# Rounding the feed-forward weights in two instructions a block, through 32-bit integers, with six of the second matrix's eight sums on ScalarE

## The chip, the core and the metric

The kernel runs on one core of one Trainium2 chip. A core has five engines that run side by side, each with its own queue of instructions: TensorE (PE in the profile; its weight loads are listed apart as PEld), VectorE (DVE), ScalarE (ACT), GpSimd (POOL) and SyncE (SP), which here only starts transfers. An engine takes its queue in order and waits on semaphores for what others produce. The metric is the device time of one execution in microseconds (us); lower is better.

## The reference

Sixteen sequences of 224 tokens with 512 features go through one gated block: cross-attention to a context of 750 rows per sequence, and then a feed-forward layer whose two weight matrices are rounded to -1, 0 and 1. What matters for this change is the rounding of the weights and where they are used:

```python
def weight_quant(w):
    scale = 1.0 / jnp.clip(jnp.mean(jnp.abs(w)), 1e-05)
    q = jnp.clip(jnp.round(w * scale), -1.0, 1.0) / scale
    return w + jax.lax.stop_gradient(q - w)

def bitlinear(x, w, b):
    xq = act_quant(rmsnorm(x))
    wq = weight_quant(w)
    return jnp.einsum('bsd,fd->bsf', xq, wq) + b
h = bitlinear(x, w1, b1)
h = jax.nn.gelu(h, approximate=False)
return bitlinear(h, w2, b2)

x = x + jnp.tanh(g_xattn[0]) * _L0_xattn_ref(_layernorm(x, axis=-1), ctx_768, mask_BxS2_bk0, ...)
x = x + jnp.tanh(g_ffn[0]) * _L0_ffn_ref(_layernorm(x, axis=-1), ...)
```

`w1` is 2048 x 512 and `w2` is 512 x 2048, both float32. A matrix can be scaled only when the mean of all its absolute values is known.

## The kernel before, in words

With these inputs the kernel takes `compact_path`. Every sequence attends to few context rows; the sequences are sorted by the number of rows that the mask keeps, and only the kept rows are fetched: at most 192 for the first eight sequences and 128 for the other eight (`CAPS`). The main loop at the end of the function runs over the sixteen sequences s. In step s it does the attention of s (`scores`, `turn_probs`, `weighted`), prepares queries, keys and values of s + 1, normalises the tokens of later sequences, and, from s = 2 on, carries pairs of 128-token tiles through the output projection and the feed-forward layer (`residual`, `project`, `normalise`, `up`, `gelu`, `down`). Steps s = 0 and s = 1 have no feed-forward work yet; in its place they prepare the weights, `w1` in step 0 and `w2` in step 1 (`weight_pieces`).

Each matrix is cut into eight blocks of 128 partitions x 1024 values. A block goes through these steps:

- `load_weights`: a transfer of 512 KB on SP's queue into a tile `raw`. There are eight such tiles, so block c of `w2` can be loaded only when block c of `w1` has been rounded out of its tile.
- `sum_weights`: the sum of absolute values of each partition, for even blocks on VectorE (L1363) and for odd ones on ScalarE (L1367). The sums of `w1` are taken ahead of the loop, those of `w2` in step 0, between the roundings of `w1`.
- `scale_weights`, once a matrix: a small matmul with ones adds over the partitions (L1375), and VectorE turns the mean into the scale (L1377 to L1386).
- `round_weights`: VectorE multiplies by the scale and cuts at 1 (L1396), cuts at -1 and writes 16-bit integers, which rounds (L1397), and turns the integers into bfloat16 (L1398). The result `w16` lies in one of three tiles with the tag `xq`.
- `turn_weights`: eight TensorE transposes (L1409 for `w1`, L1413 for `w2`) into PSUM, and an eviction to float8 into `w1T` or `w2T`.

Which engine evicts a PSUM tile is decided while the kernel is built: `evict` (L757 to L766) keeps a running sum of estimated load, `load["v"]` for VectorE and `load["s"]` for ScalarE, and gives the tile to the engine that would end lower. `round_weights` adds 1700 to `load["v"]` for each block; `sum_weights` adds nothing.

`merge` interleaves the three streams of a step (attention, preparation, weights) by their rough costs. From that the framework lays down one fixed queue per engine; neighbours can change places in it, so that in the kernel before the first instruction of block c + 1 stands ahead of the last one of block c. GpSimd's queue holds the normalisation of the tokens (L956 to L961), the fetches of tokens and context rows (L793, L856), two scalings of bias rows (L1519, L1520) and the division of the attention weights by their sum (L1081), which `turn_probs` needs before TensorE can transpose them (L1101).

Of the kernel before, what the change touches and what calls it, by code (L numbers as in the profile page):

```python
# [11 lines left out]
ALU = mybir.AluOpType  # L12
# [713 lines left out]
def compact_path(ctx, tc, sh, x, context, out, late_loads):  # L726

    nc = tc.nc
# [15 lines left out]
    I32 = mybir.dt.int32  # L744
    I16 = mybir.dt.int16
# [7 lines left out]
    load = {"v": 0.0, "s": 0.0}  # L753
# [602 lines left out]
    def sum_weights(wi, c):  # L1356
        if c == 0:
            weight_sums.append(pa.tile([P, NPC], F32, name=f"wsums_{wi}"))
        if c == 1:
            late["junk"] = pa.tile([P, FF], F32, tag="h", name=f"junk_{wi}", bufs=2)  # L1360
        raw = raws[wi, c]
        if c % 2 == 0:
            nc.vector.tensor_reduce(  # L1363
                weight_sums[wi][:, c : c + 1], raw, AX.X, ALU.add, apply_absolute_value=True
            )
        else:
            nc.scalar.activation(late["junk"][:, :W], raw, AF.Abs, accum_out=weight_sums[wi][:, c : c + 1])  # L1367

    weight_scale = [None, None]
# [22 lines left out]
    def round_weights(wi, c):  # L1392

        raw = raws.pop((wi, c))
        quantised[wi, c] = w16 = pa.tile([P, W], BF16, tag="xq", name=f"w16_{wi}_{c}", bufs=3)
        nc.vector.tensor_scalar(raw, raw, weight_scale[wi], 1.0, ALU.mult, ALU.min)  # L1396
        nc.vector.tensor_scalar(w16.bitcast(I16), raw, -1.0, None, ALU.max)  # L1397
        nc.vector.tensor_copy(w16, w16.bitcast(I16))  # L1398
        load["v"] += 1700

    def turn_weights(wi, c):
        w16 = quantised.pop((wi, c))
# [14 lines left out]
    def weight_pieces(wi):  # L1417

        p = []
        if wi == 1:  # L1420
            p += [(0.0, lambda: scale_weights(1))]
        for c in range(NPC + 2):
            if c < NPC:
                p += [(0.2, lambda c=c: round_weights(wi, c))]
                if wi == 0:
                    p += [(0.0, lambda c=c: load_weights(1, c))]
            if c > 1:
                p += [(0.6, lambda c=c: turn_weights(wi, c - 2))]
                if wi == 0:
                    p += [(0.0, lambda c=c: sum_weights(1, c - 2))]  # L1430
        return p
# [51 lines left out]
    with ExitStack() as behind:  # L1483
        for instruction in latest.values():
            behind.enter_context(tc.issue_after(instruction))
        scores(0, 0)
        scores(0, 1)
        for _, piece in queries[3:] + keys_values[3:]:
            piece()
        for c in range(NPC):  # L1490
            sum_weights(0, c)
        scale_weights(0)
        for _, piece in norm_pieces(1):
            piece()
        select(2)

        held = [sh.wo[0:1, 0, 0:1], sh.wo[0:1, 2, 0:1], sh.wo[P // 2 : P // 2 + 1, 2, 0:1]]
        for dst in held + [sh.bo[0:1, 0:1], sh.b1[0:1, 0:1], sh.b2[0:1, 0:1]]:
            nc.scalar.copy(dst, weight_sums[0][0:1, NPC - 1 : NPC])
# [85 lines left out]
```

## Time and profile before

| | |
|---|---|
| three runs | 754.46, 756.20, 758.74 us (median 756.2) |
| the profiled execution | 755.32 us, its span 753.5 us |
| TensorE | 680.1 us busy, 90% of the span |
| VectorE | 505.9 us, 67% |
| ScalarE | 407.6 us, 54% |
| GpSimd | 397.0 us, 53% |
| 43 to 160 us (weights, steps 0 to 2) | TensorE busy 105.3 of 117.0 us |
| 160 to 206 us | TensorE busy 46.0 of 46.0 us |
| 206 us to the end | TensorE busy 497.4 of 547.5 us |

The span runs from the first to the last instruction of the profile; 1.8 us of the execution's time lie around it. All other times here come from that one execution. In a list of instructions a row gives start and duration in us, engine, line, operation, what is written and read with its shape, the count, and in brackets the idle time ahead of it with what ended it. PEclk is the share of its full clock that TensorE was granted. Busy time of TensorE is modelled, so small gaps in it can be missing.

### The profile page before, as it was taken

How to read it: one execution, taken by the hardware profiler on the slowest of the kernel's cores; microseconds unless marked ns; L12 is line 12 of the kernel's file. 1: busy time of each engine (PE TensorE's matmuls, PEld its weight loads, DVE VectorE, ACT ScalarE, POOL GpSimd, SP SyncE). 2: the span in 40 equal slices, each digit the busy share in tenths (PEclk: the TensorE clock that was granted, in tenths of full speed). 3: DMA queues.
4: the chain of work that ended last, by engine and by line, in shares of the span. 5: the costliest groups of instructions: out<-in, count | busy, mean ns of one | idle time of the engine just before them, and what ended most of it. 6: DMA issues, size and time to landing. Idle time of an engine off the chain costs nothing.

```text
span 753.5 us, 11378 instructions
## 1 busy us (share of the span) xinstructions
PE 680.1 (90%) x3902; PEld 432.9 (57%) x3902; DVE 505.9 (67%) x1300; ACT 407.6 (54%) x960; POOL 397.0 (53%) x543
## 2 busy tenths in 40 slices
PE   4997799999999999997999999999999999988652
PEld 3875587666566566555655575666666666443221
DVE  5598765877484784665768676588594939586860
ACT  1556564384663855736657369266565656460530
POOL 6583567464564644647266564565654453536141
PEclk9998999999999999999999999999999999999887
DMA  6874031132223322222142323123122222213150
GB/s 193 314 267 156 11 90 45 15 73 56 69 47 70 82 56 57 67 57 81 28 99 67 71 67 68 32 77 80 58 57 70 56 70 57 71 28 77 35 113 31
DMA packets 87218, 58.77 MB, mean 78 GB/s; under 512 B 75488, under 2 KB 75632, under 8 KB 87024
## 3 DMA queue, kind: packets, MB, share of 16 engines
q1 hardware_dynamic: 79024, 32.00, 18.8%
q0 software_dynamic: 8128, 25.96, 11.1%
q8 instruction: 33, 0.54, 0.3%
q14 instruction: 33, 0.27, 0.1%
HBM read 32.26 MB, written 7.34 MB: 53 GB/s over the span
## 4 chain that ended last, share of the span: by engine, by line
PE 57%; DVE 12%; issue 10%; POOL 9%; DMA 5%; ACT 2%; POOLq 0%; ACTq 0%; DVEq 0%; SPq 0%
PE qp L1008 9%; PE op L1189 9%; PE fp L1304 8%; PE hp L1259 6%; PE kp L892 5%; PE sim L1047 4%; PE vp L907 4%; PE ptp L1101 3%; PE av L1126 3%; DVE a L1282 2%; POOL p L1081 2%; DVE h L1267 2%; DMA raw<-in_L_ffn_w_dram 2%; DMA hqT<-hq 2%; DVE hq L1285 1%
## 5 line engine op out<-in xcount | busy, mean ns | idle before, releaser
L1081 POOL TENSOR_TENSOR p<-p,rec 112x768 f32<-112x768 f32 (+1 forms) x64 | 84.2, 1318 | 74.8 <-DVE rec L1080 29.6
L1304 PE MATMUL fp<-w2T,hqT 128*128 128x512 fp8e4 x448 | 104.2, 387 | 13.8 <-DMA hqT<-hq 13.7
L1259 PE MATMUL hp<-w1T,xqT 128*128 128x512 fp8e4 x448 | 107.0, 383 | 8.8 <-DVE h L1267 6.2
L1071 ACT ACTIVATE p<-p,nm 112x192 f32<-112x192 f32 (+1 forms) x256 | 106.4, 419 | 11.5 <-DVE nm L1061 11.3
L1008 PE MATMUL qp<-xnT,wq_sb 128*128 128x224 f32 x512 | 104.9, 358 | 0.6 <-ACT xnT L766 0.6
L1189 PE MATMUL op<-wo_sb,xoT 128*128 128x512 f32 x224 | 103.7, 599 | 0.0
L1008 PEld LDWEIGHTS qp<-xnT,wq_sb 128*128 128x128 f32 x512 | 96.8, 193 | 6.4 <-issue 3.3
L1267 DVE SCALAR_TENSOR_TENSOR h<-hp,c,b_bc 128x1024 f32<-128x1024 f32 x56 | 71.6, 1280 | 39.9 <-PE hp L1259 37.4
L1061 DVE CUSTOM_DVE_ANT_0 p<-sim,mask 112x192 f32<-112x192 f32 (+1 forms) x256 | 67.7, 319 | 33.9 <-PE sim L1047 33.4
L1304 PEld LDWEIGHTS <-hqT 128*128 128x128 bf16 x448 | 43.3, 99 | 71.0 <-DMA hqT<-hq 16.9
L1282 DVE TENSOR_REDUCE a<-h 128x1 f32<-128x2048 f32 x28 | 63.9, 2282 | 22.4 <-ACT h L1279 22.3
L1259 PEld LDWEIGHTS <-xqT 128*128 128x128 bf16 x448 | 43.2, 98 | 57.7 <-issue 15.4
L1308 DVE SCALAR_TENSOR_TENSOR y<-fp,c,y 128x512 f32<-128x512 f32 x28 | 20.9, 746 | 76.3 <-PE fp L1304 73.0
L1310 POOL DMA_INDIRECT out_dram<-y,token x28 | 30.9, 1104 | 75.6 <-DVE y L1308 70.6
L1290 ACT ACTIVATE h<-h 128x2048 f32<-128x2048 f32 x28 | 53.4, 1907 | 22.1 <-DVE hq L1285 14.7
L1279 ACT ACTIVATE h<-h 128x2048 f32<-128x2048 f32 x28 | 53.5, 1909 | 19.6 <-DVE k L1200 10.6
L1189 PEld LDWEIGHTS op<-wo_sb,xoT 128*128 128x128 f32 x224 | 40.6, 190 | 38.9 <-issue 36.4
L892 PE MATMUL kp<-ctxT,wk_sb 128*128 128x192 f32 (+1 forms) x384 | 60.9, 306 | 0.0
L892 PEld LDWEIGHTS kp<-ctxT,wk_sb 128*128 128x128 f32 x384 | 55.2, 192 | 6.2 <-issue 4.3
L1247 POOL TENSOR_TENSOR y<-y,b_bc 128x512 f32<-128x512 f32 x28 | 36.6, 1311 | 37.9 <-DVE fx L1228 37.6
L766 ACT COPY pT<-ptp 128x448 f32<-128x448 f32 x63 | 32.7, 536 | 42.6 <-PE ptp L1101 41.3
L1101 PE MATMUL ptp<-ident,p 112*128 112x112 f32 x256 | 36.1, 268 | 17.6 <-POOL p L1081 17.5
(165 smaller groups left out, 1191.4 us busy)
## 6 DMA issues: line engine op xcount, KB each, us to landing
raw<-in_L_ffn_w_dram SPq DMA_DIRECT2D x16, 512.0 KB, 5.6
wq_sb<-in_L_xattn_W_q_dram SPq DMA_DIRECT2D x1, 1024.0 KB, 5.8
b_bc<-in_L_ffn_b_dram SPq DMA_DIRECT2D x1, 1024.0 KB, 7.8
wk_sb<-in_L_xattn_W_k_dram SPq DMA_DIRECT2D x1, 768.0 KB, 7.4
wv_sb<-in_L_xattn_W_v_dram SPq DMA_DIRECT2D x1, 768.0 KB, 8.8
wo_sb<-in_L_xattn_W_o_dram SPq DMA_DIRECT2D x1, 512.0 KB, 3.8
wo_sb<-in_L_xattn_W_o_dram SPq DMA_DIRECT2D x2, 256.0 KB, 5.6
x<-in_x_dram,token POOLq DMA_INDIRECT x28, 3.6
```

Source lines behind the costliest of these rows:

```text
L892: nc.tensor.matmul(pk[:, p - p0, :], lhsT=sh.wk[:, c, p * P : (p + 1) * P], rhs=st["ctxT"][:, c, :cap], start=(c == 0), stop=(c == NC - 1),)
L1008: nc.tensor.matmul(pq[:, i, :], lhsT=sh.wq[:, d, (p + i) * P : (p + i + 1) * P], rhs=st["xnT"][:, d, :], start=(d == 0), stop=(d == ND - 1),)
L1061: nc.vector.tensor_tensor_reduce(out=probs[:, h, :cap], in0=sim[:, j, i, :cap], in1=st["mask"][:, j * begin : j * begin + cap], scale=-(DH ...
L1071: nc.scalar.activation(probs[:, h, :cap], probs[:, h, :cap], AF.Exp, bias=nmax, scale=-1.0, accum_out=total[:TQ, h : h + 1],)
L1081: nc.gpsimd.tensor_tensor(probs[:, :, :cap], probs[:, :, :cap], rec[:TQ].unsqueeze(2).to_broadcast([TQ, 4, cap]), ALU.mult,)
L1101: nc.tensor.transpose(pt[:, h, :], probs[:, h, c : c + P], ident[:TQ, :TQ])
L1189: nc.tensor.matmul(po, lhsT=xoT[:, d, at : at + P], rhs=sh.wo[:, d, :], start=(d == 0), stop=(d == ND - 1))
L1259: nc.tensor.matmul(ph[:, n, :], lhsT=f["xqT"][:, k * ND + d, :], rhs=w1T[:, d, at : at + NB], start=(d == 0), stop=(d == ND - 1),)
L1267: nc.vector.scalar_tensor_tensor(h[:, cols], ph.rearrange("t i n -> t (i n)"), f["c1", k], sh.b1[:, cols], ALU.mult, ALU.add)
L1279: nc.scalar.activation(f["h", k], f["h", k], AF.Gelu)
L1282: nc.vector.tensor_reduce(amax[:, k : k + 1], h, AX.X, ALU.max, apply_absolute_value=True)
L1304: nc.tensor.matmul(po, lhsT=f["hqT", k][:, n, :], rhs=w2T[:, n, :], start=(n == 0), stop=(n == NF - 1))
```

## The change

Rounding takes two instructions a block. The first multiplies by the scale and writes the product as 32-bit integers over the block itself, which rounds it; the second reads the integers, cuts them at 1 and at -1 and writes bfloat16. The estimate that `evict` is given falls from 1700 to 1400 a block. For `w2` (`wi == 1`) only blocks 0 and 4 are summed on VectorE; blocks 1, 2, 3, 5, 6 and 7 are summed on ScalarE. For `w1` the division stays as it was, four and four.

```diff
@@ sum_weights
-        if c % 2 == 0:
+        if c % (2 + 2 * wi) == 0:
             nc.vector.tensor_reduce(
                 weight_sums[wi][:, c : c + 1], raw, AX.X, ALU.add, apply_absolute_value=True
             )
@@ round_weights
         raw = raws.pop((wi, c))
         quantised[wi, c] = w16 = pa.tile([P, W], BF16, tag="xq", name=f"w16_{wi}_{c}", bufs=3)
-        nc.vector.tensor_scalar(raw, raw, weight_scale[wi], 1.0, ALU.mult, ALU.min)
-        nc.vector.tensor_scalar(w16.bitcast(I16), raw, -1.0, None, ALU.max)
-        nc.vector.tensor_copy(w16, w16.bitcast(I16))
-        load["v"] += 1700
+        nc.vector.tensor_scalar(raw.bitcast(I32), raw, weight_scale[wi], None, ALU.mult)
+        nc.vector.tensor_scalar(w16, raw.bitcast(I32), 1.0, -1.0, ALU.min, ALU.max)
+        load["v"] += 1400
```

## The prediction

> **What bounds the kernel now.** I read the page first: TensorE is busy 90% of the span, VectorE 67%. So time taken off VectorE counts only where TensorE waits for it. The waits of TensorE from 40 to 206 us are short, and all but the last lie in the weight steps:
>
> ```profile
> PE ptp L1101 <- POOL p L1081: 5.1, 1, 5.1
> PE wp L1413 <- DVE w L1398: 3.6, 1, 3.6
> PE wp L1409 <- DVE w L1398: 1.7, 1, 1.7
> PE wtotp L1375 <- DVE wtot L1373: 1.1, 1, 1.1
> PE ptp L1101 <- ACT w2T L766: 0.2, 1, 0.2
> ```
>
> A row gives who waited for whom, the total, the count and the longest. The two waits on L1398, for the first block of each matrix, end when that block is a bfloat16 tile. The longest, 57.8 to 62.9 us, ends when GpSimd has divided the probabilities (L1081). From 103.3 to 206 us TensorE hardly waits. Time won before 103 us should therefore reach 206 us, and from there too, if what follows hangs on TensorE's own results.
>
> Why L1081 is late shows in GpSimd's instructions in order of time:
>
> ```profile
> 45.43 1.51 POOL L959 TENSOR_SCALAR ls_x<-mv_x 128x2 f32<-128x2 f32 x1
> 46.93 4.52 POOL L1519 TENSOR_SCALAR bo_bc<-bo_bc,tgates 128x512 f32<-128x512 f32 x1
> ...
> 61.36 2.90 POOL L1081 TENSOR_TENSOR p<-p,rec 112x768 f32<-112x768 f32 x2
> ```
>
> From 44.8 to 61.4 us this queue has hardly a gap. L959 takes 0.19 us elsewhere and L1519's twin L1520 1.55 us: here they lose 1.3 and 3.0 us. VectorE in the same stretch, and in the second one:
>
> ```profile
> 45.21 0.74 DVE L1396 TENSOR_SCALAR raw<-raw,sw 128x1024 f32<-128x1024 f32 x1
> 45.88 0.41 DVE L1398 CAST w<-w 128x1024 bf16<-128x1024 int16 x1
> ...
> 49.41 0.68 DVE L1397 TENSOR_SCALAR w<-raw 128x1024 int16<-128x1024 f32 x1
> 50.01 0.34 DVE L1061 CUSTOM_DVE_ANT_0 p<-sim,mask 112x192 f32<-112x192 f32 x1
> ...
> 60.45 4.10 DVE L1398 CAST w<-w 128x1024 bf16<-128x1024 int16 x2
> ...
> 87.06 0.68 DVE L1397 TENSOR_SCALAR w<-raw 128x1024 int16<-128x1024 f32 x1
> 87.66 0.75 DVE L1396 TENSOR_SCALAR raw<-raw,sw 128x1024 f32<-128x1024 f32 x1
> 88.33 0.84 DVE L1398 CAST w<-w 128x1024 bf16<-128x1024 int16 x1
> ```
>
> It rounds without a break until 50.0 us; then comes an instruction of another kind, and L1519 ends 1.4 us later. At 60.45 it is the other way round: two casts stretch to 4.1 us until L1081 is done. The last view is busy time by stretches that I laid on the clock's steps:
>
> ```profile
> 58.40:61.81 3.41, 0.00 (x0) 0.00 (x0) 3.41 (x7) 3.39 (x6) 2.78 (x4) 1.00 0.90 254
> 61.81:65.22 3.41, 2.33 (x12) 1.44 (x12) 3.41 (x2) 0.75 (x3) 2.45 (x2) 0.50 0.86 302
> ...
> 85.70:89.12 3.42, 0.00 (x0) 0.00 (x0) 3.42 (x12) 0.58 (x1) 3.23 (x5) 1.00 0.00 0
> 89.12:92.53 3.41, 3.30 (x17) 2.96 (x18) 3.41 (x6) 1.88 (x4) 2.36 (x3) 0.50 0.00 0
> ```
>
> Columns: the stretch, its length, busy PE, PEld, DVE, ACT, POOL, and then the clock. After a stretch without matmuls TensorE runs at half clock: until 68.6 us, and until 92.5 us. Each gap so costs more than its length.
>
> [...] 1024 values take 0.74 (f32 to f32), 0.68 (f32 to int16) and 0.41 us (int16 to bf16), the full-rate sum L1363 1.21. No row has 1024 int32 values. [...] steps near 61.8, 68.6, 89.1 and 92.5 us are multiples of 3.41 us apart.
>
> **The change part by part.**
>
> *Rounding.* It removes 16 casts x 0.66 = 10.5 us of VectorE (a mean with holds; undisturbed 0.41, queue to queue 0.33). The other two stay two: for int32 I take [...]0.74 and 0.68 us. Bounds: as now, or full rate, 1.21 each by L1363.
>
> *First wait of step 0.* Block 0 is ready when L1397 ends, at 45.3 instead of 46.3 us: 1.0 us. TensorE then works without a wait until 57.8, now 56.9 us, and meets L1081 anyway: by itself this is worth nothing.
>
> *The wait on L1081.* In the changed order six rounding instructions stand between 44.6 us and VectorE's first L1061, three of each kind, which follow each other (start to start) after 0.60 and 0.66 us: 3.8 us, so L1061 starts at 48.4 instead of 50.0 and lets L1519 in 1.6 us sooner. Behind L1519 stand L780, L1520, two L961, a context fetch, two token fetches, another fetch, and L1081: the same durations put L1081 at 59.8 instead of 61.36. Its other inputs are early: rec at 55.25 us, or sooner. But the fetches now meet a denser run[...], as the sum of block 2 no longer lies between; one fetch of 1.0 us took 1.38 in such company, another 1.02. I take 1.5; bounds 0 (the holds eat it) and 3.1 (L1519 slips in at an earlier boundary). The gap falls from 5.1 to about 4.5 us[...]: the half clock after it stays.
>
> *First block of w2.* L1396, the small L1386 and L1397 keep their order; the block is ready when L1397 ends, 87.74 us, and not at 89.18 with the cast held by GpSimd: 1.4 us. TensorE is then idle 85.65 to 87.8, 2.15 us, with 1.0 us of work in the 2 us ahead, so [...]the half clock probably stays away. The transposes, 1.03 us instead of 0.6, and what follows until 92.5 us then go at full clock; the next keys (L892) start at 89.65 instead of 91.6, held a little by ScalarE's evictions, and end 2.4 us sooner in all. Bounds: 1.4 with the half clock, 2.6 without that hold.
>
> *Sums.* VectorE loses 2 x 1.21 = 2.4 us, ScalarE gains 2 x (1.06 + 0.19) = 2.5 us in step 0. Cost nothing: ScalarE was busy 12.0 of the 20 us from 62 to 82. Behind them on its queue stand evictions of w1T and pT; by my count the first comes at 62.2, when the changed TensorE finishes the transposes for it. Without that cover each costs up to 1.25 us. The loads wait for the last read of each raw tile, which is no later; they land in 3.8 to 7.1 us.
>
> *Evictions.* The changed orders, compared engine by engine, show 16 casts and two sums fewer on VectorE and two evictions more in net, two fewer on ScalarE, between steps 0 and 3. TensorE's, GpSimd's and SP's queues keep theirs, and from then on all do. From 110 to 206 us TensorE sets the pace, so I cost this at nothing. The later fetches of y (L793 at 105.45) wait for the last L1397 and come some 5 us sooner, more than TensorE's 3.9: the division at 121.8, just in time now, stays in time.
>
> Sum: 1.5 + 2.4 = 3.9 us, on the profiled 755.3 gives 751.4. The median is 0.9 us above that execution[...], and I take 751.8.
>
> **The rivals.** 0.5% of 756.2, about what a measurement of this kernel can tell, is 3.8 us.
>
> *GpSimd gains nothing.* The denser run holds the fetches by what the shorter one freed; the half clock returns in step 1. Left are 1.4 us: 754. For it speaks L961 at 87.16 us, 3.16 us for two of 0.76; against it the fetches at 57.7 and 59.0, [...]at 1.0 us.
>
> *The clock helps twice.* L1519 slips in early, [...]its half clock, 5.7 us long, goes too: 3.1 + 2.8 + 2.4 = 8.3, 747. Nothing promises that slip; the trace shows it missed six boundaries.
>
> *int32 at full rate*, so the change doesn't do what it says: 16 x 2 x about 0.5 = 16 us more against 10.5 saved. [...]block 0 of w2 is ready 0.5 us sooner, L1061 of step 1 some 2 us later: about 755.[...]
>
> *Slower: GpSimd starved.* If each dense run holds GpSimd whole, as 44.6 to 50 us did, the runs over blocks 4 to 6 of w1 hold it 2.5 + 1.25 us; less 1.6, L1081 starts 2.1 us late. In step 1 the run of six after 87.7 us, 3.8 us, puts the division at 100.2 late by as much; TensorE has 0.16 us to spare there. 5.9 us more: 761. It wins once the holds exceed some 5.5 of these 7.5 us. For it speaks L1519, against it the fetches.
>
> **How the numbers follow.** Forecast 0.56, with a range of its own of 749.5 to 753.5 and three quarters of it below 752.4; GpSimd gains nothing 0.18; clock twice 0.13; full rate 0.04; starved 0.09. Faster by over 0.5%: 0.42 + 0.13 = 0.55. Within: 0.14 + 0.18 + 0.04 = 0.36. Slower: 0.09. The range of 748 to 757 leaves out the starved case and half of the best one.
>
> **What would show it.** Right: no casts; int32 rows of 0.74 and 0.68 us; L1519 well under 4.5 us; L1081 of step 0 at about 59.8; first transposes of w2 at about 86.3 (87.8 less the 1.5 won before), at full clock; VectorE near 494 us busy, ScalarE near 409. Wrong: int32 rows above 1 us; L1081 after 61.4; a wait of TensorE for an eviction by ScalarE at 61 to 66 us; or a gap after 206 us that gives the time back, as where GpSimd's fetches and half clocks (one follows 351.9 us) decide[...].

## The result, and the profile after

The changed kernel takes 753.5 us (median of 22 runs, 750.9 to 756.6), the kernel before 757.3 us in the same comparison (22 runs, 753.6 to 762.7). The ratio is 0.9951, with a 95% interval of 0.9933 to 0.9968: 0.5% faster, or 3.7 us, with 2.4 and 5.1 us as its ends. The forecast was 4.4 us below the earlier median, 751.8. The profiled execution took 753.5 us with a span of 751.7.

The head of the page after, with busy times and counts of instructions:

```profile
span 751.7 us, 11370 instructions
...
PE 683.9 (91%) x3902; PEld 437.4 (58%) x3902; DVE 497.0 (66%) x1284; ACT 407.4 (54%) x962; POOL 397.3 (53%) x543
```

VectorE has 16 instructions fewer and 8.9 us less work; ScalarE and GpSimd are where they were. TensorE does the same 3902 matmuls in 3.8 us more, as more of them ran at half clock (the mean granted clock is 0.969, before 0.976; from 40 to 206 us half clock lasts 13.7 us, before 10.2). Lines behind L1398 now count one less (L1409 is L1408, L1413 is L1412, L1519 is L1518, L1520 is L1519).

The waits of TensorE from 40 to 206 us (who for whom, total, count, longest):

```profile
PE ptp L1101 <- POOL p L1081: 4.2, 2, 3.0
PE wp L1412 <- DVE w L1397: 2.1, 1, 2.1
PE wtotp L1375 <- DVE wtot L1373: 1.1, 1, 1.1
PE wp L1408 <- DVE w L1397: 0.7, 1, 0.7
...
```

The first block of `w2` is waited for 2.1 instead of 3.6 us, the first of `w1` 0.7 instead of 1.7, and step 0's division 3.0 instead of 5.1. The second wait of the first row, 1.15 us ending at 204.77, isn't new: before, it stands at 206.96 us with 0.95, just outside the stretch. A table cut at a fixed time can lose a wait in one kernel and show it in the other.

VectorE in order of time, at the start of step 0:

```profile
43.70 0.73 DVE L1396 TENSOR_SCALAR raw<-raw,sw 128x1024 int32<-128x1024 f32 x1
...
45.12 0.67 DVE L1397 TENSOR_SCALAR w<-raw 128x1024 bf16<-128x1024 int32 x1
45.72 1.40 DVE L1396 TENSOR_SCALAR raw<-raw,sw 128x1024 int32<-128x1024 f32 x2
...
48.91 0.34 DVE L1061 CUSTOM_DVE_ANT_0 p<-sim,mask 112x192 f32<-112x192 f32 x1
```

Both new forms take no longer than the float ones before: 0.73 and 0.67 us (in step 1 0.73 and 0.68), against 0.74 for f32 to f32 and 0.68 for f32 to int16; the sum over as many values, L1363, takes 1.22. L1061, the first instruction of another kind, comes at 48.91 instead of 50.01.

GpSimd in the same stretch:

```profile
46.49 3.97 POOL L1518 TENSOR_SCALAR bo_bc<-bo_bc,tgates 128x512 f32<-128x512 f32 x1
...
60.42 2.89 POOL L1081 TENSOR_TENSOR p<-p,rec 112x768 f32<-112x768 f32 x2
```

L1518 is still held until after L1061 has started, 3.97 us where its twin L1519 takes 1.56, and ends at 50.46 instead of 51.45; the division starts at 60.42 instead of 61.36. These differences are too small as they stand: the start-up differs from one execution to the next, and the first scaling on VectorE falls at 43.19 before and at 43.70 after. The rows to count from and to, before and then after (L1413, now L1412, is the first transpose of `w2`, L1126 the first product of probabilities and values in step 1):

```profile
43.19 0.73 DVE L1396 TENSOR_SCALAR raw<-raw,sw 128x1024 f32<-128x1024 f32 x1
...
89.23 1.03 PE L1413 MATMUL wp<-ident,w 128*128 128x128 bf16 x8 [3.57 <-DVE w L1398]
...
110.23 1.74 PE L1126 MATMUL av<-pT,v 128*64 128x224 f32 x16
```

```profile
85.50 1.03 PE L1412 MATMUL wp<-ident,w 128*128 128x128 bf16 x8 [2.15 <-DVE w L1397]
...
107.56 1.73 PE L1126 MATMUL av<-pT,v 128*64 128x224 f32 x16
```

Counted from the first scaling, the division comes at 18.17 before and 16.72 after, 1.45 us sooner, and L1126 at 67.04 and 63.86, 3.2 us sooner. From there to the end it takes 643.3 before and 644.2 after. So the gain is made in the weight steps, and most of it lasts.

Between these rows the gain isn't even. The small matmul L1375 ahead of `w2` comes 2.8 us sooner (38.80 instead of 41.62), the first transpose of `w2` 4.2 us sooner, and L1126 only 3.2: step 0 gave 2.8 us, the first block of `w2` 1.4, and 1.1 were lost again behind it, where half clock now lasts longer.

The last view is busy time by stretches on the clock's steps (stretch, length, busy PE, PEld, DVE, ACT, POOL, then the clock):

```profile
60.25:63.66 3.41, 1.71 (x15) 1.15 (x16) 1.74 (x2) 3.41 (x6) 3.04 (x3) 1.00 0.91 259
63.66:67.07 3.41, 3.41 (x23) 2.74 (x21) 2.07 (x7) 2.09 (x5) 0.00 (x0) 0.50 0.66 198
80.73:84.14 3.41, 1.50 (x14) 0.98 (x11) 3.25 (x20) 3.01 (x12) 2.17 (x4) 1.00 0.00 0
84.14:87.55 3.41, 2.05 (x13) 1.71 (x14) 3.41 (x6) 0.98 (x2) 3.30 (x3) 0.50 0.00 0
```

TensorE falls to half clock at 63.66 and at 84.14 us, though it was at work for about half of the stretch ahead of each. The second half clock lasts until 90.96 us.

### The profile page after: what moved, and what is told of

Read it like the earlier page. It is cut to its first block, busy times and chain, and to the rows that moved or that the text cites. A ratio compares the mean times of both kernels' runs of the same rounds, so it can differ in the third digit from the quotient of the medians.

```text
span 751.7 us, 11370 instructions
## 1 busy us (share of the span) xinstructions
PE 683.9 (91%) x3902; PEld 437.4 (58%) x3902; DVE 497.0 (66%) x1284; ACT 407.4 (54%) x962; POOL 397.3 (53%) x543
## 4 chain that ended last, share of the span: by engine, by line
PE 52%; issue 14%; DVE 13%; POOL 12%; DMA 4%; ACT 3%; POOLq 0%; DVEq 0%; ACTq 0%; SPq 0%
PE qp L1008 9%; PE op L1189 9%; PE fp L1304 6%; PE hp L1259 5%; PE kp L892 5%; PE sim L1047 4%; PE vp L907 4%; DVE a L1282 3%; PE ptp L1101 3%; POOL p L1081 2%; DVE h L1267 2%; PE av L1126 2%; DMA hqT<-hq 2%; POOL out_dram L1310 2%; POOL y L793 1%
## 5 line engine op out<-in xcount | busy, mean ns | idle before, releaser
L1081 POOL TENSOR_TENSOR p<-p,rec 112x768 f32<-112x768 f32 (+1 forms) x64 | 83.7, 1310 | 74.3 <-DVE rec L1080 42.0
L1061 DVE CUSTOM_DVE_ANT_0 p<-sim,mask 112x192 f32<-112x192 f32 (+1 forms) x256 | 67.5, 318 | 38.4 <-PE sim L1047 35.7
L892 PE MATMUL kp<-ctxT,wk_sb 128*128 128x192 f32 (+1 forms) x384 | 64.7, 318 | 0.0
L892 PEld LDWEIGHTS kp<-ctxT,wk_sb 128*128 128x128 f32 x384 | 59.0, 202 | 6.2 <-issue 4.3
L1047 PE MATMUL sim<-kT,qT 64*112 64x192 f32 (+1 forms) x512 | 51.1, 316 | 0.4 <-DVE h L1267 0.4
```

The costliest lines, as they stand in the source:

```text
L892: nc.tensor.matmul(pk[:, p - p0, :], lhsT=sh.wk[:, c, p * P : (p + 1) * P], rhs=st["ctxT"][:, c, :cap], start=(c == 0), stop=(c == NC - 1),)
L1047: nc.tensor.matmul(sim[:, j, i, :cap], lhsT=st["qT"][j * DH : (j + 1) * DH, p, q * TQ : (q + 1) * TQ], rhs=st["kT"][j * DH : (j + 1) * DH, ...
L1061: nc.vector.tensor_tensor_reduce(out=probs[:, h, :cap], in0=sim[:, j, i, :cap], in1=st["mask"][:, j * begin : j * begin + cap], scale=-(DH ...
L1081: nc.gpsimd.tensor_tensor(probs[:, :, :cap], probs[:, :, :cap], rec[:TQ].unsqueeze(2).to_broadcast([TQ, 4, cap]), ALU.mult,)
```

## The experiments

Theory: the rounding makes the gain, since one instruction, which stood ahead of the transposes and in the runs beside which GpSimd's rows are held (L1519 for 4.52 us before), is gone from each block; sums and evictions cost nothing. Rivals: the sums or the moved evictions have a part in it; VectorE's time as such counts; a clock that fell otherwise made the difference. All ratios are to the kernel before in the same comparison.

**The two parts, each alone.**

```diff
-        nc.vector.tensor_scalar(raw, raw, weight_scale[wi], 1.0, ALU.mult, ALU.min)
-        nc.vector.tensor_scalar(w16.bitcast(I16), raw, -1.0, None, ALU.max)
-        nc.vector.tensor_copy(w16, w16.bitcast(I16))
-        load["v"] += 1700
+        nc.vector.tensor_scalar(raw.bitcast(I32), raw, weight_scale[wi], None, ALU.mult)
+        nc.vector.tensor_scalar(w16, raw.bitcast(I32), 1.0, -1.0, ALU.min, ALU.max)
+        load["v"] += 1400
```

> The new rounding with the old division of w2's sums (four and four). Theory (the rounding does it all, through the ready first block and through GpSimd's queue): like the full change, 0.995 of before; GpSimd's division of step 0 starts 1.3 to 1.6 us earlier than in the kernel before, measured from the first scaling on VectorE. Rival (the moved sums carry part of it): 0.9975 or above, and that division not earlier than half of this.

```diff
-        if c % 2 == 0:
+        if c % (2 + 2 * wi) == 0:
```

> The old rounding in three instructions with the new division of w2's sums (two and six). Theory: within 0.2% of before, as no wait of TensorE hangs on a sum. Rival (the sums carry part): 0.9975 or below. If ScalarE's longer queue costs something, above 1.002.

The rounding alone: 0.9942 (0.9923 to 0.9962), as much as the whole change. The sums alone: 1.0015 (0.9986 to 1.0044), no difference. In the profile of the rounding alone the first block of `w2` is waited for 2.1 us, but the division, expected 1.3 to 1.6 us sooner, gains nothing: it starts 18.40 us after the first scaling. GpSimd and VectorE there:

```profile
58.68 2.89 POOL L793 DMA_INDIRECT x<-in_x_dram,token  x1 [0.30 <-issue]
...
62.84 2.90 POOL L1081 TENSOR_TENSOR p<-p,rec 112x768 f32<-112x768 f32 x2
```

```profile
62.65 3.65 DVE L1396 TENSOR_SCALAR raw<-raw,sw 128x1024 int32<-128x1024 f32 x1
```

A token fetch, 1.0 us in the median, lasted 2.89 beside VectorE's run and ended at 61.57, just after a sum had begun there (L1363, 61.51), and then the next scaling, beside the division, took 3.65 us, 2.9 more than the 0.73 elsewhere. The hold that the rival "GpSimd gains nothing" named is real, then. This fetch cost 1.9 us; in the profile of the whole change the longer of the two ahead of the division took 1.52, half a us more than undisturbed. L1126 of step 1 still comes 2.3 us sooner than before, at 64.74: 1.4 us by the first block of `w2` and 0.9 by step 0, where half clock after the division lasts 3.4 instead of 6.8 us. So in this execution the gain didn't come from an earlier division.

**GpSimd's queue.** The two bias rows are scaled by ScalarE instead of by GpSimd, in the kernel before and in the changed one.

```diff
-                nc.gpsimd.tensor_scalar(sh.bo, sh.bo, sh.tgates[:, 0:1], None, ALU.mult)
-                nc.gpsimd.tensor_scalar(sh.b2, sh.b2, sh.tgates[:, 1:2], None, ALU.mult)
+                nc.scalar.activation(sh.bo, sh.bo, AF.Copy, scale=sh.tgates[:, 0:1])
+                nc.scalar.activation(sh.b2, sh.b2, AF.Copy, scale=sh.tgates[:, 1:2])
```

> The kernel before, with the two scalings of bias rows moved from GpSimd to ScalarE, where they stand ahead of the evictions of step 0. Theory (the queue on GpSimd[...] sets the long wait of TensorE in step 0): the 4.5 + 1.55 us of the two scalings leave that queue, the division of step 0 starts when its sums are there, some 5 us earlier, the gap of 5.1 us and the half clock after it shrink or go, 748 to 752, 0.99 to 0.995. Rival (VectorE's time sets it, GpSimd's queue has slack): the division starts within 1 us of where it was, ratio 0.998 to 1.002.

> The changed kernel with the same move. Theory: both gains in part add[...], 745 to 750, 0.985 to 0.992 of before. Rival (both shorten the same wait[...]): no better than the changed kernel, 0.994 to 0.996.

On the kernel before: 0.9943 (0.9922 to 0.9964), with the rounding left as it was. On the changed one: 0.9917 (0.9884 to 0.9949). The waits of TensorE in the first of them:

```profile
PE wp L1413 <- DVE w L1398: 3.6, 1, 3.6
...
PE ptr L1108 <- ACT w1T L766: 0.6, 1, 0.6
...
PE ptp L1101 <- POOL p L1081: 0.3, 1, 0.3
...
```

The wait for the division is nearly gone, and with it 0.6%: GpSimd's queue did cost time before. The division starts 2.8 us sooner and not the 5 expected (15.35 us after the first scaling), and its second half waits 1.98 us for VectorE. A small wait for an eviction by ScalarE shows that ScalarE isn't free at that place. The second of these kernels has 7 runs only; its interval reaches into that of the changed kernel. And the hold stays, at another row of GpSimd's queue: here L959, a row of 0.19 us with the extra copy, took 5.57.

**A third instruction put back.** Both kernels have the whole change, and one more VectorE instruction a block. In one it is a copy of the block onto itself, 0.41 us, which stands ahead of the transposes; in the other it is a sum over 256 columns, which takes the same 0.41 us and which no transpose waits for.

```diff
+        nc.vector.tensor_copy(w16, w16)
```

> The changed kernel with a third instruction a block again: a copy of the rounded block onto itself, about 0.4 us, [...]ahead of the block's transposes. Nothing of the result changes. Theory (the saved instruction is the gain: 1.4 us at the first block of w2, the rest in GpSimd's queue): most of it goes, 0.9975 to 1.000 of before; the first transposes of w2 wait 3.3 to 3.6 us again. Rival (the gain comes from the int32 form or the sums): stays at 0.994 to 0.996.

```diff
+        nc.vector.tensor_reduce(small(f"xs_{wi}_{c}")[:, 0:1], w16[:, :256], AX.X, ALU.add)
```

> The changed kernel with a sum over 256 columns of the rounded block in the same place, about as long as that copy, [...]for which no transpose waits. Its result isn't used. Theory ([...]the ready block count, not VectorE's time): 0.993 to 0.997, first transposes of w2 after 2.1 to 2.5 us, and GpSimd's instructions from 45 to 52 us held less than in the run with the copy. Rival (VectorE's time counts): like the run with the copy.

With the copy: 1.0000 (0.9976 to 1.0024), all of the gain undone. With the sum: 0.9953 (0.9927 to 0.9978), all of it kept; the two intervals overlap only at their ends. GpSimd's rows, with the copy and then with the sum:

```profile
46.26 6.96 POOL L1519 TENSOR_SCALAR bo_bc<-bo_bc,tgates 128x512 f32<-128x512 f32 x1
...
62.94 2.89 POOL L1081 TENSOR_TENSOR p<-p,rec 112x768 f32<-112x768 f32 x2
```

```profile
48.02 1.68 POOL L1519 TENSOR_SCALAR bo_bc<-bo_bc,tgates 128x512 f32<-128x512 f32 x1
...
60.20 1.47 POOL L1081 TENSOR_TENSOR p<-p,rec 112x768 f32<-112x768 f32 x1
```

The copy lengthens the unbroken run, and L1519 waits through ten of VectorE's instructions in a row, from 47.27 to 52.67 us, and ends at 53.22, once L1061 has come between. With the sum, L1519 is recorded from 48.02 us, while the first of the sums runs (47.90 to 48.31), and passes in 1.68 us. Why the copy holds GpSimd and the sum doesn't was not shown. Counted from the first scaling the division starts at 18.76 with the copy and 14.98 with the sum; of these 3.8 us, 1.7 are a longer pause of VectorE ahead of its run (2.10 against 0.43 us); TensorE was at half clock there in the first profile, from 42.0 us. The ratios, from 14 and 22 runs, don't rest on that. In the waits of TensorE the first block of `w2`, copy and then sum:

```profile
PE wp L1413 <- DVE w L1398: 3.6, 1, 3.6
```

```profile
PE wp L1413 <- DVE w L1397: 2.1, 1, 2.1
```

The sum's 0.41 us on VectorE's queue cost nothing (0.9953, and 0.9951 without it): L1519 wasn't held, and the wait for `w2` stayed at 2.1 us. With the copy L1519 took 6.96 us and that wait 3.6, so the pair doesn't say how the copy's loss divides between the two; an instruction that only delays the transposes, or only holds GpSimd, wasn't tried.

**The evictions.** The estimate for a rounding goes back to 1700 in the changed kernel.

```diff
-        load["v"] += 1400
+        load["v"] += 1700
```

> The changed kernel with the estimate of each rounding put back from 1400 to 1700, so that the evictions are given out much as in the kernel before; nothing else. My reading (the evictions cost nothing, the rounding gives all): 0.993 to 0.997 of the time before, as the whole change, with VectorE some 495 to 498 us busy. Rival (the lower estimate moves evictions to VectorE where ScalarE was late, and part of the gain is theirs): 0.998 or above. Opposite rival (those evictions delay VectorE's roundings): 0.992 or below. In the waits of TensorE the wait for the division and the one for the first block of w2 stay within 0.5 us of 4.2 and 2.1.

0.9953 (0.9934 to 0.9972), the ratio of the whole change: where the evictions went had no part in the gain that this comparison could show. The expected wait for the division, within 0.5 us of 4.2, was missed: 1.1 us, in one wait. Half clock lasted from 40.80 to 54.45 us in this execution, so TensorE came later; its index sums came later too, VectorE waited 2.45 us for one of them, and GpSimd went through that pause:

```profile
45.83 1.57 POOL L1518 TENSOR_SCALAR bo_bc<-bo_bc,tgates 128x512 f32<-128x512 f32 x1
```

**The first block of w2.** `scale_weights(1)` moves from the start of step 1 to the end of step 0, in the changed kernel, and then in the one with its bias rows on ScalarE.

```diff
-        if wi == 1:
-            p += [(0.0, lambda: scale_weights(1))]
         for c in range(NPC + 2):
...
+        if wi == 0:
+            p += [(0.0, lambda: scale_weights(1))]
```

> The changed kernel with the scale of w2 taken at the end of step 0 instead of the start of step 1, so that its first blocks are rounded while TensorE still has the scores of that step to do. Theory (the wait for w2's first block and the half clock behind it still cost 2.1 + 1.1 us and 1.7 to 3.4 us): those waits go, 747 to 751, 0.987 to 0.992 of before. Rival (a wait for probabilities takes their place, as the scores now come later): 0.993 to 0.998.

> That and the bias rows on ScalarE together. Theory: both waits of TensorE in the weight steps are gone, 742 to 748, 0.980 to 0.988 of before. Rival as before it: 0.990 to 0.994, no better than the bias rows alone.

Scaled early: 0.9898 (0.9865 to 0.9932), 751.0 us, from 6 runs. With both, expected at 0.980 to 0.988: 0.9918 (0.9893 to 0.9943), 752.1 us, no better than either edit alone. All waits of TensorE of 40 to 206 us, first with the early scale, then with both:

```profile
PE ptp L1101 <- POOL p L1081: 7.8, 4, 4.8
PE wp L1408 <- DVE w L1397: 1.2, 1, 1.2
```

```profile
PE ptp L1101 <- POOL p L1081: 5.4, 5, 1.4
PE wp L1408 <- DVE w L1397: 0.7, 1, 0.7
```

The wait for `w2` and the one for the sum are gone, 3.3 us that the change had left. In their place stand more waits for the division: in five places with both edits. GpSimd doesn't come sooner by the early scale: counted from the first scaling, the division of step 0 starts at 16.72 us without it and 17.44 with it, and with the bias rows on ScalarE at 13.03 and 13.24. This would explain why the edits don't add. In total TensorE waited no less with the early scale, 9.0 us against 8.5 in the changed kernel; what is less in that profile is half clock, 6.8 us against 13.7 (table below). The early scale is the fastest kernel here; it wasn't timed against the changed kernel in one comparison, and their intervals against the kernel before only just don't overlap.

**The same kernel once more.** The changed kernel, with no edit, in a second profile.

> The changed kernel unaltered, for a second profile: which of the readings of its first profile belong to the kernel and which to one execution. My reading: the int32 rows (0.73 and 0.68 us), the wait of some 2.1 us for the first block of w2 and the division starting 16 to 17.5 us after the first scaling belong to the kernel; where the clock halves doesn't[...]: in another execution its steps fall elsewhere against the kernel, and the half clock after the first block of w2 (84.1 to 91.0 us in the first profile) may be absent, shorter, or elsewhere. Rival (the steps follow from the kernel's gaps alone): half clock again from about 84 to 91 us and from 46.6 to 50.

750.9 us, a span of 749.0. The rows of 0.73 and 0.67 us, the wait of 2.1 us for `w2`, and L1518 with 3.97 us are the same; the division starts 16.05 us after the first scaling. Busy time by stretches, columns as above:

```profile
81.28:84.69 3.41, 1.27 (x14) 1.03 (x14) 3.41 (x12) 1.15 (x2) 3.16 (x5) 1.00 0.00 0
84.69:88.10 3.41, 3.41 (x13) 3.41 (x12) 3.41 (x7) 1.23 (x4) 3.24 (x2) 0.50 0.00 0
```

Half clock follows the wait for `w2` here too, but for one stretch instead of two; after the division, waited for 2.3 us, there is none. The first L1126 of step 1 comes 60.83 us after the first scaling, 3.0 us sooner than in the first profile of the same code. Of what I expected of this half clock (absent, shorter or elsewhere) it was shorter: place and length vary, its coming didn't.

Found the same way, in stretches of a quarter of a us, half clock between 40 and 206 us, in us:

| kernel | wait for w2 | half clock |
|---|---|---|
| before | 3.6 | 61.8-68.6, 89.1-92.5 |
| sums alone | 3.6 | 46.2-53.1, 87.2-94.0 |
| before, bias on ScalarE | 3.6 | 47.4-54.3, 85.0-91.8 |
| extra copy | 3.6 | 42.0-52.2, 65.8-69.3, 86.3-93.2 |
| after | 2.1 | 46.6-50.0, 63.7-67.1, 84.1-91.0 |
| after, once more | 2.1 | 47.1-50.6, 84.7-88.1 |
| estimate 1700 | 2.1 | 40.8-54.5, 85.2-92.0 |
| rounding alone | 2.1 | 47.1-50.6, 64.2-67.6, 88.1-91.5 |
| after, bias on ScalarE | 2.1 | 45.5-49.0, 83.1-86.5 |
| extra sum | 2.1 | 47.2-50.6, 84.7-88.1 |
| after, scaled early | none | 62.6-69.4 |
| both | none | none |

## Why the prediction was right, and where it was wrong

The forecast was 3.9 us by its sum; the comparison gives 3.7, between 2.4 and 5.1. The mechanism held: the rounding makes the gain, by what waits for it and not by VectorE's time. That the total fell so near is partly luck, since in the first profile one term was too small and the other too large. Point by point:

*Rounding: right.* For int32 0.74 and 0.68 us were foreseen, 0.73 and 0.67 measured. VectorE came to 497 instead of 494 us, and not by the roundings: L1396 and L1397 took 0.6 us less than the same two lines before. Evictions that moved to VectorE add 2.4 us in net, and the rows of L816 took 2.2 us more.

*First wait of step 0: right.* 1.7 became 0.7 us. That this is worth nothing by itself wasn't tried alone.

*The wait on L1081: right on the division, short on what it is worth.* 1.5 us sooner was foreseen, through L1061 and L1519 coming 1.6 sooner; counted from the first scaling they came 1.6 and 1.5 us sooner, and the division 1.45. The second profile gave 2.1 us, that of the rounding alone a loss of 0.2 to a held fetch: the spread given to this term, 0 to 3.1, was needed, and its lower end just missed. The gap of 4.5 us was wrong: 3.0 and 2.3 us, because TensorE itself was held up by a half clock from 46.6 us (47.1 in the second profile) which the profile of before happens not to have. Nine of the twelve profiles in the table have a half clock that begins by 47.4 us; the forecast leaned on one of the three without. The half clock after it, said to stay, lasted 3.4 instead of 6.8 us in the first profile and was absent in the second. With that, step 0 gave 2.8 and 5.0 us up to L1375, not 1.5 (0.9 with the rounding alone). How much of this the change made can't be read from one profile of before: the kernel with the sums alone, whose time is that of before, reaches L1375 1.7 us sooner than before (39.94 after the first scaling), and it too had no half clock after the division.

*First block of w2: half right.* 1.4 us sooner and an idle time of 2.15 us were foreseen, and measured as 3.57 less 2.15, 1.42. The step that failed is the next one, "the half clock probably stays away". It came in each of the six profiles with a wait of 2.1 us, 3.4 or 6.8 us long, though TensorE's work filled 44% of the stretch ahead of 84.14 us. So the term was at most 1.4, its lower bound, and not 2.4; in the first profile the longer half clock took 1.1 of it back. The forecast of 751.8 lies half a us below what its sum leaves of the median, 752.3, by an estimate that some executions before lack this half clock; that was not shown, and all four profiles with a wait of 3.6 us have it. The terms as foreseen on their own, 1.45 for the division and 1.4 here, make 2.9 us; that is inside the measured interval, but the runs of one kernel spread by 6 us and can't tell 2.9 from 3.9.

*Sums and evictions: right.* Each cost nothing by its own run, the sums within 0.14% below and 0.44% above.

*From 103 us on: right in the main.* 0.9 of 3.2 us was lost on the way to the end.

Of the rivals, "the clock helps twice" had the wrong picture: in the second profile no half clock followed the gap of step 0, 2.3 us long, without L1519 (now L1518, 3.97 us) slipping in early. "GpSimd starved" needed 5.5 us of new holds; with the rounding alone, the worst case seen, the two token fetches ahead of the division lost 0.5 + 1.9 = 2.4 us, and in step 1 TensorE didn't wait for the division at all. "Full rate" is refuted by the rows, 0.73 and 0.67 us instead of 1.21.

## What to carry to other kernels

When an instruction is taken out of a dense VectorE run beside which GpSimd's rows are held (here 3.97 to 6.96 us for a scaling of 1.6), its own time may count for little (0.41 us a block more on VectorE cost nothing here); ask what on GpSimd waits for the run to break, and what on TensorE waits for the chain that the instruction stood in. Where several such waits lie one behind the other, each edit alone may bring half a per cent and two together no more, because the next wait is already due (here 0.9951 for the change, 0.9917 with the bias rows on ScalarE, 0.9898 scaled early, 0.9918 with both). One profile gives the durations of rows (0.73 and 0.67 us in both of the changed kernel), but not how long the clock is halved (13.7 us in one, 6.8 in the other, between 40 and 206 us): take two profiles of the same kernel before a term of a sum rests on it.

## What the runs showed of the hardware

**The clock halves after stretches that were far from empty.** Inside one run the steps of the granted clock lie at whole multiples of 3.41 us from one another, as 46.59, 50.00, 63.66, 67.07, 84.14 and 90.96 us after. The stretches of 3.41 us ahead of the halvings were 50% (63.66), 44% (84.14) and 81% (46.59) busy by the profile's modelled time, and 97% with the extra copy (41.95). Other such stretches of the changed kernel, 61% busy from 56.83 us and 57% from 251.39, kept the full clock, so the modelled busy share isn't what decides. Nor does it help to set transposes and one-column matmuls aside. What remains is 0% ahead of 46.59 us and 19% ahead of 84.14, while a stretch of before with 13% (44.74 to 48.15 us) kept the full clock. What decides stays open.

**A hold is not settled at the next end of an instruction.** In a run of VectorE's roundings most instructions end within 0.75 us, but the GpSimd instruction beside it went on waiting through several of them: 3.97 (after), 4.52 (before) and 6.96 us (extra copy) for the same scaling; 1.57 where VectorE paused (estimate 1700) and 1.68 where a sum lay in the run (extra sum). Nor did it pass where it started first: with the extra copy VectorE was idle from 44.91 to 47.01 us, L1519 is recorded from 46.26 and was still caught by the run after it (spans on GpSimd are rough, so its true start may be later). Which instruction is caught varies from one execution to the next, also where the code ahead is the same: L959 took 0.19 us in two profiles (extra copy, estimate 1700) and 0.58 (after), 1.51 (before), 3.95 (scaled early), 5.56 (sums alone) and 5.57 us (before, bias on ScalarE) in others.
